# Two of four heads' softmax sums taken four slots at a time from SBUF, with a third buffer of logits and an earlier start of the statistics

## The chip, the cores and the metric

The kernel runs on one core of one Trainium2 chip. The metric is the device time of one execution in microseconds, and a version is given by the median of its runs. A profiled execution lies beside the timed ones: its span is what the trace covers, and its own device time is that span and the little around it.

## What is computed

The input is two images of 256 channels and 64 x 64 = 4096 positions. Two residual layers follow one another, each behind a group normalisation: a Mamba block (layer 0) and an attention of 8 heads with 32 channels each (layer 1). Everything is in float32.

```
# layer 0: x = x + mamba(group_norm(x))
# layer 1: x = x + attention(group_norm(x))
qkv = einsum('bchw,oc->bohw', x, qkv_w) + qkv_b
q, k, v = ...                                  # [b, head, 32, 4096] each
attn_logits = einsum('bhci,bhcj->bhij', q, k) / sqrt(32)
attn_weights = softmax(attn_logits, axis=-1)
out = einsum('bhij,bhcj->bhci', attn_weights, v)
```

The kernel leaves the maximum of the softmax out. It takes the exponential of the scaled logits, multiplies it with the values, sums the exponentials over the 4096 keys, and divides at the end. A check at the end of the kernel (`out_of_range`) sends inputs for which this would overflow to another routine, which does not run here.

## The kernel before

**Layer 0** is one stage for both images (`mamba_stage`). Its work is written as tasks with an engine, a due time and a cost, and a planner (`Plan`) orders them before anything is issued. What is written outside the planner is issued first, in the order of the text: on the queue of SP all weights and vectors (`load_rows`, `load_vec`, lines 327 to 354), about 3.7 MB. Then come the planner's tasks. `first` (line 313) loads one tile of 512 positions of an image into the ring `r_h` (five buffers) and takes `bn_stats` of it on VectorE; it is called for the 8 tiles of image 0 and of image 1. `group_norm` (line 405) makes the scales of the normalisation from an image's statistics, and `front(0)` starts the first tile of the Mamba block with a second load of the same input (`yn`, line 459).

**Layer 1** is done image by image (`attention_block`). `prepare` projects queries, keys and values and stores queries and keys in DRAM. Then comes the main loop, whose order is written out by hand. The heads go in two groups of four; a tile is one group and 512 queries; a slot is 128 keys of one tile. So a tile has 32 slots, an image has 2 x 8 x 32 = 512, and both have 1024. In a slot:

- TensorE makes logits for four heads as two halves of two heads (`logits`, line 964). A half fills a PSUM tile `s` of 128 x 1024[...]. The pool `ps_s` has two such buffers.
- ScalarE takes the exponential of a half in one instruction (`exponentials`, line 972) and writes it to SBUF (`e`, a ring of seven buffers).
- TensorE multiplies the four heads' exponentials with the values and accumulates over the tile in PSUM (`values`, line 981, tile `po`[...]).
- The exponentials are summed over the slots (`add_up`, line 990). The first half is added by VectorE to `acc`[...] (line 1002). The second half is added by GpSimd to `acc_p` in SBUF (line 1013); in the slots named by `SHARED` (every second one from slot 6, 13 in a tile) VectorE takes one head of it into `acc_2`[...] (lines 1008 and 1010), and GpSimd the other (line 1011).

At the end of a tile `finish` (line 1015) runs as a generator, one piece per slot beside the next tile's slots: copies of `acc` and `po` to SBUF, the sum over the 128 keys of a slot by a matmul with ones (line 1031), reciprocals, the product, and the residual.

With two logit buffers the loop is skewed by half a slot. In slot s ScalarE takes the second half of slot s and the first half of slot s + 1, and TensorE does the values of slot s - 1, then the second half of logits of slot s + 1 and the first half of slot s + 2:

```
                exponentials(s, 1)
                exponentials(s + 1, 0)
...
                values(s - 1)
...
            logits(s + 1, 1)
            logits(s + 2, 0)
            if s < S:
                add_up(s)
```

Of the kernel before, what the change touches and what calls it, by code (L numbers as in the profile page):

```python
# [11 lines left out]
F32 = mybir.dt.float32  # L12
F32R = mybir.dt.float32r
AF = mybir.ActivationFunctionType
ALU = mybir.AluOpType
# [4 lines left out]
P = 128  # L20
# [226 lines left out]
def mamba_stage(ctx, tc, xs, stats_out, consts, w, outs):  # L247
# [65 lines left out]
    def first(b, t, due):  # L313
        xt = Buf(r_h)
        add("SP", due, 0.8, lambda: nc.sync.dma_start(xt.tile, image_tile(xs[b], t)), [], [xt], lands=3.0)
        for k in range(KC):
            add(
                "DVE",
                due,
                0.7,  # L320
                lambda k=k: nc.vector.bn_stats(stats_in[b][:, k, t, :], xt.tile[:, k, :]),
                [xt],
                [stats_bufs[b][k * NT + t]],
            )

# [13 lines left out]
    w_in = load_rows("w_in", w["W_inT"], KC)  # L339
    conv_w = wp.tile([P, KD, TAPS], F32, name="conv_w")  # L340
    nc.sync.dma_start(conv_w, w["conv_w"].rearrange("(k p) o t -> p k (o t)", p=P))
    conv_b = load_vec("conv_b", w["conv_b"], KD)
    w_xp = load_rows("w_xp", w["W_xpT"], KD)
    b_dt = load_vec("b_dt", w["b_dt"], KD)
    d_vec = load_vec("d_vec", w["D"], KD)
    neg_a = wp.tile([P, KD, QUAD, NQ], F32, name="neg_a")
    nc.sync.dma_start(neg_a, w["A_log"].rearrange("p (k j q) -> p k j q", k=KD, j=QUAD))
    sum4 = wp.tile([P, PQ], F32, name="sum4")
    nc.sync.dma_start(sum4, w["sum4"])
    w_out = load_rows("w_out", w["W_outT"], KD)  # L350
    w_1 = load_rows("w_1", w["W1T"], KC)
    b_1 = load_vec("b_1", w["b1"], KH)
    w_2 = load_rows("w_2", w["W2T"], KH)
    b_2 = load_vec("b_2", w["b2"], KC)
# [5 lines left out]
    diag_d = wp.tile([P, KD, P], F32, name="diag_d")  # L360
    perm = r_yn.make()[:, 0, 0:P]
    nc.sync.dma_start(perm, w["perm"])
    for k in range(KD):
# [10 lines left out]
    pick = wp.tile([NS, NQ, P], F32R, name="pick")  # L374
    w_dt32 = r_yn.make()[:R, 0, :]
    nc.sync.dma_start(w_dt32, w["W_dtT"])
# [4 lines left out]
    pick32 = r_yn.make()[:NS, 0, :]  # L381
    nc.sync.dma_start(pick32, w["pick"])
# [5 lines left out]
    r_proj.make = itertools.cycle(projs).__next__  # L388


# [374 lines left out]
    for b in range(IMAGES):  # L765
        for t in range(NT):
            first(b, t, -60 + 10 * b)
    for b in range(IMAGES):
        for k in range(KC):
            group_norm(b, k, -48 + 10 * b)  # L770
    front(0)
# [42 lines left out]
def attention_block(ctx, tc, b, stats, consts, w, out, scratch, range_t):  # L814
# [14 lines left out]
    wp = ctx.enter_context(tc.tile_pool(name=f"l1w{b}", bufs=1))  # L829
    ps_s = ctx.enter_context(tc.tile_pool(name=f"l1pss{b}", bufs=2, space=PSUM))  # L830
    ps_a = ctx.enter_context(tc.tile_pool(name=f"l1psa{b}", bufs=1, space=PSUM))
    ps_2 = ctx.enter_context(tc.tile_pool(name=f"l1ps2{b}", bufs=1, space=PSUM))
# [109 lines left out]


    class Slot:
        pass

    S = KG * NT * NC
    SHARED = range(6, NC, 2)
    todo = {}
# [19 lines left out]
    def exponentials(s, half):  # L969
        if s < S:  # L970
            e = ep.tile([P, 2, T], F32, name="e")
            nc.scalar.activation(e, todo[s].s[half], AF.Exp, scale=SCALE)  # L972
            todo[s].e.append(e)

    def values(s):
        i, c = divmod(s, NC)
        g = i // NT
        if c == 0:
            tiles[i].po = ps_o.tile([P, T], F32, name="po")
        for h in range(4):  # L980
            nc.tensor.matmul(  # L981
                tiles[i].po[h * D : (h + 1) * D, :],
                lhsT=v[:, c, g * P + h * D : g * P + (h + 1) * D],
                rhs=todo[s].e[h // 2][:, h % 2, :],
                start=(c == 0),
                stop=(c == NC - 1),
            )
        del todo[s]

    def add_up(s):  # L990

        i, c = divmod(s, NC)
        tile_ = tiles[i]
        ea, eb = todo[s].e
# [7 lines left out]
        nc.vector.tensor_add(acc, acc, ea)  # L1002
        if c == 1:
            nc.gpsimd.tensor_add(acc_p, tile_.eb0, eb)  # L1004
        elif c in SHARED:
            if c == SHARED[0]:
                tile_.acc_2 = ps_2.tile([P, T], F32, name="acc_2", tag="a2")
                nc.vector.tensor_copy(tile_.acc_2, eb[:, 0, :])
            else:
                nc.vector.tensor_add(tile_.acc_2, tile_.acc_2, eb[:, 0, :])  # L1010
            nc.gpsimd.tensor_add(acc_p[:, 1, :], acc_p[:, 1, :], eb[:, 1, :])  # L1011
        else:
            nc.gpsimd.tensor_add(acc_p, acc_p, eb)  # L1013

    def finish(i):
# [34 lines left out]
    with tc.manual_schedule():  # L1050
        logits(0, 0)
        logits(0, 1)
        exponentials(0, 0)
        logits(1, 0)
# [201 lines left out]
```

## Time and profile before

| what | us |
|---|---|
| median of 3 runs (4609.26 to 4615.61) | 4610.98 |
| the profiled execution's own time | 4614.82 |
| its span | 4613.0 |

The stages, read from the busy time of the engines by stretch (us busy in each):

| stretch of the span, us | what runs | PE | VectorE | ScalarE | GpSimd |
|---|---|---|---|---|---|
| 0 to 45 | loads, statistics of both images | 0.0 | 27.2 | 1.5 | 2.7 |
| 45 to 112 | group norm, front of the first tiles | 56.0 | 12.1 | 35.9 | 10.2 |
| 112 to 2090 | Mamba block, both images | 1779.9 | 1804.7 | 1585.1 | 1906.8 |
| 2090 to 2194 | prepare, image 0 | 92.1 | 43.5 | 28.2 | 0.0 |
| 2194 to 3336 | attention, image 0 | 1142.0 | 889.2 | 989.9 | 978.8 |
| 3336 to 3452 | prepare, image 1 | 97.2 | 52.0 | 29.2 | 3.2 |
| 3452 to 4594 | attention, image 1 | 1142.0 | 887.2 | 989.4 | 977.8 |
| 4594 to 4613 | last tile's end, check | 2.4 | 9.4 | 0.0 | 3.6 |

A matmul's end is modelled in the trace and includes time in which it stands behind others, so TensorE's 1142.0 us in the attention stretches do not say that it always had work; the distance between the starts of matmuls does. GpSimd is the busiest engine of the Mamba block (1906.8 of 1978 us).

### The profile page before, as it was taken

Reading aid. Unit: us, or ns where it says so; the run is one execution under the profiler, and the core shown is the slowest. Engines: PE = TensorE matmul, PEld = TensorE weight load, DVE = VectorE, ACT = ScalarE, POOL = GpSimd, SP = SyncE. Lnnn points to the kernel's source line nnn. Section 1 sums busy time; section 2 is a strip of 40 time slices with the busy share of each in tenths; the row PEclk is TensorE's granted clock in tenths of the full one; section 3 lists DMA queues with packets and bytes.
Section 4 is the critical chain, followed back from the end, with each engine's and each line's share of the span. In section 5 each row is a group of like instructions: output and inputs, shape, how many; then the busy total and the mean of one; then the engine's idle time right before and its main releaser. Section 6 shows DMA issues by size and latency. Waiting matters only on the chain.

```text
span 4613.0 us, 55891 instructions
## 1 busy us (share of the span) xinstructions
PE 4311.6 (93%) x18530; PEld 1571.9 (34%) x18530; DVE 3725.3 (81%) x3980; ACT 3659.2 (79%) x4796; POOL 3883.1 (84%) x2251
## 2 busy tenths in 40 slices
PE   4799899999999999888999999999989999999998
PEld 2233333333333333324333333333343333333332
DVE  3999999999999999963777777777747777777777
ACT  3778888888888888752888888888828888888887
POOL 1999999999999999960888888888808888888887
PEclk9899999999999999989999999999999999999999
DMA  5333333333333333318210140101081101401000
GB/s 172 105 107 111 108 122 119 123 124 124 124 124 111 119 124 122 108 41 256 77 44 17 26 101 17 26 17 29 7 262 37 44 17 28 99 17 26 24 23 8
DMA packets 162329, 379.66 MB, mean 82 GB/s; under 512 B 23408, under 2 KB 41584, under 8 KB 153840
## 3 DMA queue, kind: packets, MB, share of 16 engines
q1 hardware_dynamic: 162032, 376.03, 26.6%
q8 instruction: 147, 2.41, 0.2%
q14 instruction: 150, 1.23, 0.1%
HBM read 282.64 MB, written 93.32 MB: 81 GB/s over the span
## 4 chain that ended last, share of the span: by engine, by line
PE 65%; POOL 11%; DVE 10%; issue 6%; ACT 3%; DMA 3%; SPq 0%; POOLq 0%; DVEq 0%; ACTq 0%
PE s L964 27%; PE po L981 22%; DVE h L721 6%; POOL h L727 6%; PE mm L403 6%; POOL dbu L716 3%; PE y L753 2%; PE mm L599 2%; PE mm L635 2%; PE s L887 1%; DVE bn L716 1%; DMA xn<-x_dram 1%; PE bn L403 1%; ACT da L710 1%; DMA dtu_rep<-dtu_dram 1%
## 5 line engine op out<-in xcount | busy, mean ns | idle before, releaser
L972 ACT ACTIVATE e<-s 128x1024 f32<-128x1024 f32 x2048 | 1987.1, 1022 | 305.2 <-PE s L964 305.0
L1002 DVE TENSOR_TENSOR acc<-acc,e 128x1024 f32<-128x1024 f32 x992 | 1219.4, 1229 | 407.5 <-ACT e L972 404.4
L1013 POOL TENSOR_TENSOR acc_p<-acc_p,e 128x1024 f32<-128x1024 f32 x544 | 1300.4, 2390 | 235.0 <-ACT e L972 222.5
L964 PE MATMUL s<-q,k 128*128 128x512 f32 x4096 | 1317.4, 435 | 3.8 <-ACT e L972 2.1
L727 POOL TENSOR_TENSOR h<-h,c 128x1024 f32<-128x1024 f32 x512 | 1206.5, 2370 | 15.4 <-ACT state L724 10.0
L981 PE MATMUL po<-e,v 128*32 128x512 f32 x8192 | 1092.0, 605 | 0.0
L964 PEld LDWEIGHTS s<-q,k 128*128 128x128 f32 x4096 | 614.0, 188 | 1120.2 <-ACT e L972 1114.5
L710 ACT ACTIVATE da<-dt_rep,neg_a 128x512 f32<-128x512 f32 x1024 | 691.3, 701 | 119.8 <-DVE h L721 98.0
L721 DVE TENSOR_TENSOR_SCAN h<-da,state,dbu 128x512 f32<-128x512 f32 x512 | 649.9, 1274 | 81.3 <-POOL dbu L716 72.1
L721 DVE TENSOR_TENSOR_SCAN h<-da,state,bn 128x512 f32<-128x512 f32 x512 | 647.6, 1265 | 13.7
L1011 POOL TENSOR_TENSOR acc_p<-acc_p,e 128x512 f32<-128x512 f32 x416 | 548.0, 1317 | 33.0 <-POOL acc_p L1013 0.6
L716 POOL TENSOR_TENSOR dbu<-dtu_rep,b 128x512 f32<-128x512 f32 x384 | 488.1, 1282 | 10.0 <-DMA dtu_rep<-dtu_dram 8.4
L234 ACT ACT_TABLE_LOAD x331 | 424.7, 1283 | 6.7 <-PEq L1246 0.7
L403 PE MATMUL bn<-proj,pick 112*128 112x512 f32 x512 | 307.6, 616 | 118.3 <-DVE h L721 117.9
L753 PE MATMUL y<-h,sum 128*32 128x512 f32 x2048 | 379.9, 638 | 40.2 <-POOL h L727 40.1
L716 DVE TENSOR_TENSOR bn<-dtu_rep,bn 128x512 f32<-128x512 f32 x512 | 348.9, 681 | 34.8 <-DMA dtu_rep<-dtu_dram 19.1
L1010 DVE TENSOR_TENSOR acc<-acc,e 128x512 f32<-128x512 f32 x384 | 268.7, 700 | 58.5 <-ACT e L972 37.8
L1004 POOL TENSOR_TENSOR acc_p<-e 128x1024 f32<-128x1024 f32 x32 | 76.4, 2387 | 273.5 <-ACT e L972 273.5
L981 PEld LDWEIGHTS po<-e,v 128*32 128x32 f32 x8192 | 161.6, 108 | 373.2 <-issue 361.9
L403 PE MATMUL mm<-yn,w_in 128*128 128x512 f32 x512 | 264.5, 642 | 10.0 <-ACT yn L492 4.5
L403 PE MATMUL mm<-xm,taps 128*128 128x512 f32 x512 | 235.5, 603 | 16.4 <-POOL xm L539 14.2
L403 PE MATMUL mm<-yn,w 128*128 128x512 f32 x512 | 239.1, 596 | 11.5 <-ACT z L587 10.2
(125 smaller groups left out, 3444.6 us busy)
## 6 DMA issues: line engine op xcount, KB each, us to landing
dt_rep<-dt_dram SPq DMA_DIRECT2D x128, 512.0 KB, 5.0
dtu_rep<-dtu_dram SPq DMA_DIRECT2D x128, 512.0 KB, 5.7
qk_dram<-halves SPq DMA_DIRECT2D x64, 512.0 KB, 5.9
q<-qk_dram SPq DMA_DIRECT2D x128, 256.0 KB, 4.8
k<-qk_dram SPq DMA_DIRECT2D x64, 512.0 KB, 7.6
b<-bc_dram SPq DMA_DIRECT2D x64, 256.0 KB, 3.0
c<-bc_dram SPq DMA_DIRECT2D x64, 256.0 KB, 4.1
dt_dram<-dt SPq DMA_DIRECT2D x64, 256.0 KB, 2.0
```

Source lines behind the costliest of these rows:

```text
L403: nc.tensor.matmul(out, lhsT=lhsT, rhs=rhs, start=(i == 0), stop=(i == len(pairs) - 1))
L710: nc.scalar.activation(da[j].tile, dt.tile[:, j, :], AF.Exp, scale=scale)
L716: engine.tensor_mul(out.tile, dtu.tile[:, j, :], rows.tile)
L721: nc.vector.tensor_tensor_scan(h.tile[:, j, :], da[j].tile, dbu.tile, initial, ALU.mult, ALU.add)
L727: nc.gpsimd.tensor_tensor(h.tile, h.tile, rows_c.tile.unsqueeze(1).to_broadcast([P, 2, T]), ALU.mult)
L753: nc.tensor.matmul(y.tile[j * PQ : (j + 1) * PQ, :], lhsT=sum4, rhs=pair[j // 2].h.tile[:, j % 2, :], start=False, stop=(qd == NQ - 1),)
L964: nc.tensor.matmul(ps[:, j, :], lhsT=keys[i // NT, kt][:, h, kj : kj + P], rhs=queries[i][:, h, :], start=True, stop=True)
L972: nc.scalar.activation(e, todo[s].s[half], AF.Exp, scale=SCALE)
L981: nc.tensor.matmul(tiles[i].po[h * D : (h + 1) * D, :], lhsT=v[:, c, g * P + h * D : g * P + (h + 1) * D], rhs=todo[s].e[h // 2][:, h % 2, :],
L1002: nc.vector.tensor_add(acc, acc, ea)
L1011: nc.gpsimd.tensor_add(acc_p[:, 1, :], acc_p[:, 1, :], eb[:, 1, :])
L1013: nc.gpsimd.tensor_add(acc_p, acc_p, eb)
```

## The change

In the attention:

- `acc` in PSUM is gone, and `ps_s` has three buffers of logits instead of two. The skew of half a slot goes with it: slot s takes both halves of its own exponentials, and TensorE makes both halves of slot s + 1.
- The first half's exponentials are no longer added slot by slot. Four slots' exponentials are written into one SBUF tile `chunk` of five parts of 128 x 1024 (two such tiles). After the fourth slot one `tensor_reduce` on VectorE adds the parts: the four new ones and part 0, the running sum of the chunks before. It writes its result into part 0 of the next chunk. The first reduction of a tile has four terms, the next six have five, and the last one, in `finish`, has five and writes to `acc_sb` directly. The read is made by `rearrange("p k h t -> p (h t) k")`: the innermost step goes from part to part, that is 1024 elements or 4096 bytes at a time.
- The ring `e` serves the second half alone and has five buffers instead of seven.
- `SHARED` has 15 slots of a tile instead of 13 (from slot 8 those whose number has the remainder 0, 2, 4, 5 or 6 by 8).
- `finish` copies `po` first, then reduces, and waits five slots instead of one before the matmul with ones.

At the start of the kernel:

- The loads and statistics of image 0 are issued before all weights, outside the planner. Image 1's stay tasks, with a later due time.
- `w_out`, `w_1` and `w_2` are loaded by one late task of the planner; some small loads change their places.

```diff
+    with tc.manual_schedule():
+        for t in range(NT):
+            first(0, t, 0)
...
+    def load_late():
+        for tile_, name in ((w_out, "W_outT"), (w_1, "W1T"), (w_2, "W2T")):
+            nc.sync.dma_start(tile_, w[name].rearrange("(k p) f -> p k f", p=P))
...
-        for t in range(NT):
-            first(b, t, -60 + 10 * b)
+        for t in range(NT if b else 0):
+            first(b, t, -30)
...
-            group_norm(b, k, -48 + 10 * b)
+            group_norm(b, k, -48 + 24 * b)
+    add("SP", -20, 2.4, load_late, [], [late_buf], lands=12.0)
...
-    ps_s = ctx.enter_context(tc.tile_pool(name=f"l1pss{b}", bufs=2, space=PSUM))
-    ps_a = ctx.enter_context(tc.tile_pool(name=f"l1psa{b}", bufs=1, space=PSUM))
+    ps_s = ctx.enter_context(tc.tile_pool(name=f"l1pss{b}", bufs=3, space=PSUM))
...
-    ep = ctx.enter_context(tc.tile_pool(name=f"l1e{b}", bufs=7))
+    CHUNK = 4
+    ep = ctx.enter_context(tc.tile_pool(name=f"l1e{b}", bufs=5))
+    ec = ctx.enter_context(tc.tile_pool(name=f"l1c{b}", bufs=2))
...
-    SHARED = range(6, NC, 2)
+    SHARED = [c for c in range(8, NC) if c % 8 in (0, 2, 4, 5, 6)]
...
     def exponentials(s, half):
-        if s < S:
+        c = s % NC
+        if half == 0:
+            if c % CHUNK == 0:
+                todo[s].chunk = todo.pop("chunk", None) or chunk()
+            else:
+                todo[s].chunk = todo[s - 1].chunk
+            e = todo[s].chunk[:, 1 + c % CHUNK]
+        else:
             e = ep.tile([P, 2, T], F32, name="e")
-            nc.scalar.activation(e, todo[s].s[half], AF.Exp, scale=SCALE)
-            todo[s].e.append(e)
+        nc.scalar.activation(e, todo[s].s[half], AF.Exp, scale=SCALE)
+        todo[s].e.append(e)
+
+    def chunk():
+        return ec.tile([P, 1 + CHUNK, 2, T], F32, name="chunk")
+
+    def sum_chunk(s, out):
+        first = 1 if s % NC < CHUNK else 0
+        terms = todo[s].chunk.rearrange("p k h t -> p (h t) k")[:, :, first:]
+        nc.vector.tensor_reduce(out.rearrange("p h t -> p (h t)"), terms, AX.X, ALU.add)
...
     def add_up(s):
...
+        if c % CHUNK == CHUNK - 1 and c < NC - 1:
+            todo["chunk"] = chunk()
+            sum_chunk(s, todo["chunk"][:, 0])
         if c == 0:
-            tile_.acc = ps_a.tile([P, 2, T], F32, name="acc")
             tile_.acc_p = p2.tile([P, 2, T], F32, name="acc_p")
-            nc.vector.tensor_copy(tile_.acc, ea)
             tile_.eb0 = eb
             return
-        acc, acc_p = tile_.acc, tile_.acc_p
-        nc.vector.tensor_add(acc, acc, ea)
+        acc_p = tile_.acc_p
...
-        acc = p1.tile([P, 3, T], F32, name="acc_sb")
-        nc.vector.tensor_copy(acc[:, 0:2, :], d.acc)
-        nc.vector.tensor_add(acc[:, 2, :], d.acc_2, d.acc_p[:, 0, :])
         po = p1.tile([P, T], F32, name="po_sb")
         nc.vector.tensor_copy(po, d.po)
+        acc = p1.tile([P, 3, T], F32, name="acc_sb")
+        sum_chunk(i * NC + NC - 1, acc[:, 0:2])
+        nc.vector.tensor_add(acc[:, 2, :], d.acc_2, d.acc_p[:, 0, :])
...
-        yield
+        yield 5
...
-                exponentials(s + 1, 0)
+                exponentials(s, 0)
...
+            logits(s + 1, 0)
             logits(s + 1, 1)
-            logits(s + 2, 0)
```

More of the change, by code (lines that the diff above doesn't have):

```diff
@@ L314, in first @@
         xt = Buf(r_h)
-        add("SP", due, 0.8, lambda: nc.sync.dma_start(xt.tile, image_tile(xs[b], t)), [], [xt], lands=3.0)
-        for k in range(KC):
[L317 to L324, printed above, removed]
+        load = lambda: nc.sync.dma_start(xt.tile, image_tile(xs[b], t))
+        stats = lambda k: nc.vector.bn_stats(stats_in[b][:, k, t, :], xt.tile[:, k, :])
+        if b == 0:
+            xt.tile = r_h.make()
+            load()
+            for k in range(KC):
+                stats(k)
+            return
+        add("SP", due, 0.8, load, [], [xt], lands=3.0)
+        for k in range(KC):
+            add("DVE", due, 0.7, lambda k=k: stats(k), [xt], [stats_bufs[b][k * NT + t]])
+    with tc.manual_schedule():
+        for t in range(NT):
+            first(0, t, 0)
     def load_rows(name, src, k):
@@ L338, in mamba_stage @@
     beta = load_vec("beta", w["beta"], KC)
-    w_in = load_rows("w_in", w["W_inT"], KC)
     conv_w = wp.tile([P, KD, TAPS], F32, name="conv_w")
@@ L342, in mamba_stage @@
     conv_b = load_vec("conv_b", w["conv_b"], KD)
+    w_in = load_rows("w_in", w["W_inT"], KC)
     w_xp = load_rows("w_xp", w["W_xpT"], KD)
     b_dt = load_vec("b_dt", w["b_dt"], KD)
-    d_vec = load_vec("d_vec", w["D"], KD)
     neg_a = wp.tile([P, KD, QUAD, NQ], F32, name="neg_a")
     nc.sync.dma_start(neg_a, w["A_log"].rearrange("p (k j q) -> p k j q", k=KD, j=QUAD))
+    w_dt32 = r_yn.make()[:R, 0, :]
+    nc.sync.dma_start(w_dt32, w["W_dtT"])
+    pick32 = r_yn.make()[:NS, 0, :]
+    nc.sync.dma_start(pick32, w["pick"])
+    d_vec = load_vec("d_vec", w["D"], KD)
+    perm = r_yn.make()[:, 0, 0:P]
+    nc.sync.dma_start(perm, w["perm"])
     sum4 = wp.tile([P, PQ], F32, name="sum4")
     nc.sync.dma_start(sum4, w["sum4"])
-    w_out = load_rows("w_out", w["W_outT"], KD)
-    w_1 = load_rows("w_1", w["W1T"], KC)
     b_1 = load_vec("b_1", w["b1"], KH)
-    w_2 = load_rows("w_2", w["W2T"], KH)
     b_2 = load_vec("b_2", w["b2"], KC)
@@ L360, in mamba_stage @@
     diag_d = wp.tile([P, KD, P], F32, name="diag_d")
-    perm = r_yn.make()[:, 0, 0:P]
-    nc.sync.dma_start(perm, w["perm"])
     for k in range(KD):
@@ L374, in mamba_stage @@
     pick = wp.tile([NS, NQ, P], F32R, name="pick")
-    w_dt32 = r_yn.make()[:R, 0, :]
-    nc.sync.dma_start(w_dt32, w["W_dtT"])
     for row in (0, LOW):
@@ L380, in mamba_stage @@
         nc.vector.tensor_sub(w_dt[rows, 1, :], w_dt32, w_dt[rows, 0, :].bitcast(F32))
-    pick32 = r_yn.make()[:NS, 0, :]
-    nc.sync.dma_start(pick32, w["pick"])
     nc.vector.tensor_copy(pick.rearrange("r q p -> r (q p)"), pick32)
@@ L388, in mamba_stage @@
     r_proj.make = itertools.cycle(projs).__next__
+    w_out, w_1, w_2 = (
+        wp.tile([P, k, C if name != "w_1" else HID], F32, name=name)
+        for name, k in (("w_out", KD), ("w_1", KC), ("w_2", KH))
+    )
+    late_buf = Buf()
+    def load_late():
+        for tile_, name in ((w_out, "W_outT"), (w_1, "W1T"), (w_2, "W2T")):
+            nc.sync.dma_start(tile_, w[name].rearrange("(k p) f -> p k f", p=P))
     state = wp.tile([P, IMAGES, KD, QUAD, NQ], F32, name="state")
@@ L987, in values @@
             )
-        del todo[s]
     def add_up(s):
@@ L993, in add_up @@
         tile_ = tiles[i]
-        ea, eb = todo[s].e
+        eb = todo[s].e[1]
+        if c % CHUNK == CHUNK - 1 and c < NC - 1:
+            todo["chunk"] = chunk()
+            sum_chunk(s, todo["chunk"][:, 0])
         if c == 0:
-            tile_.acc = ps_a.tile([P, 2, T], F32, name="acc")
             tile_.acc_p = p2.tile([P, 2, T], F32, name="acc_p")
-            nc.vector.tensor_copy(tile_.acc, ea)
             tile_.eb0 = eb
             return
-        acc, acc_p = tile_.acc, tile_.acc_p
-        nc.vector.tensor_add(acc, acc, ea)
+        acc_p = tile_.acc_p
         if c == 1:
@@ L1052, in attention_block @@
         logits(0, 1)
-        exponentials(0, 0)
-        logits(1, 0)
         s = 0
```

## Prediction

> **What bounds the kernel now.** I read the stages first, then the costliest groups, then the waits and TensorE's timeline in the attention, which takes half the span, and the timeline of the start.
>
> ```profile
> L972 ACT ACTIVATE e<-s 128x1024 f32<-128x1024 f32 x2048 | 1987.1, 1022 | 305.2 <-PE s L964 305.0
> L1002 DVE TENSOR_TENSOR acc<-acc,e 128x1024 f32<-128x1024 f32 x992 | 1219.4, 1229 | 407.5 <-ACT e L972 404.4
> L1013 POOL TENSOR_TENSOR acc_p<-acc_p,e 128x1024 f32<-128x1024 f32 x544 | 1300.4, 2390 | 235.0 <-ACT e L972 222.5
> ...
> L1011 POOL TENSOR_TENSOR acc_p<-acc_p,e 128x512 f32<-128x512 f32 x416 | 548.0, 1317 | 33.0 <-POOL acc_p L1013 0.6
> ...
> L1010 DVE TENSOR_TENSOR acc<-acc,e 128x512 f32<-128x512 f32 x384 | 268.7, 700 | 58.5 <-ACT e L972 37.8
> ```
>
> No engine but TensorE is full: ScalarE waits for logits (305 us), the adders wait for exponentials. The waits from 3560 to 4500 us name the partner:
>
> ```profile
> PEld s L964 <- ACT e L972: 457.2, 827, 0.8
> ...
> ACT e L972 <- PE s L964: 125.0, 421, 1.2
> ```
>
> Logits wait for the exponentials that free their buffer, and exponentials for logits: a loop through two buffers. TensorE's timeline shows its price:
>
> ```profile
> 4002.82 1.07 PE L981 MATMUL po<-e,v 128*32 128x512 f32 x8
> 4003.82 1.19 PE L964 MATMUL s<-q,k 128*128 128x512 f32 x4
> 4004.94 1.07 PE L981 MATMUL po<-e,v 128*32 128x512 f32 x8
> 4005.93 1.38 PE L964 MATMUL s<-q,k 128*128 128x512 f32 x4
> 4007.24 0.64 PE L981 MATMUL po<-e,v 128*32 128x512 f32 x4
> ```
>
> Slots last 2.12 us (4002.82 to 4004.94) and 2.30 us in turn. In the short one values (1.00) and four logits (1.12) follow each other closely; in the long one the second pair of logits came late. Value matmuls start at 3451.57 in the first tile of image 1 and at 4526.20 in the last: 71.64 us a tile of 32 slots, of which the sums of a finished tile make one slot 2.9 to 3.0 us. At the start:
>
> ```profile
> 22.83 6.03 DVE L321 BATCH_NORM_STATS2 stats_in<-h 128x6 f32<-128x512 f32 x10
> ...
> 37.06 8.05 DVE L321 BATCH_NORM_STATS2 stats_in<-h 128x6 f32<-128x512 f32 x12 [0.74 <-DMA h<-in_x]
> ...
> 45.02 0.59 DVE L412 BATCH_NORM_AGGREGATE gn<-stats_in 128x2 f32<-128x48 f32 x2
> ...
> 48.26 1.50 ACT L457 ACTIVATE yn<-yn,scales 128x512 f32<-128x512 f32 x2
> ```
>
> Image 0's scales wait until VectorE has taken image 1's statistics too, behind 3.7 MB of weights.
>
> [...] 512 elements take 676 ns, close to the 700 of an add:
>
> ```profile
> L1043 DVE TENSOR_REDUCE range_t<-r 128x1 f32<-128x512 f32 x32 | 21.6, 676 | 0.0
> ```
>
> [...] No strided read of such length is in the trace.
>
> **The change part by part.**
>
> *TensorE.* The instructions stay. With three buffers the first half of slot s+1's logits goes to the buffer of the exponential before the last slot's end, the second to that of this slot's first exponential, which ends long before. The values need the last slot's exponentials. ScalarE needs 1.94 us for its two (timeline), less than 2.12. So every slot can be a short one: 32 x 2.12 = 67.8, and the sums matmul adds 2.96 - 2.12 = 0.84: 68.7 us a tile. The gain is 71.6 - 68.7 = 2.9 a tile, 32 tiles: 93 us; I take 88, for the shorter first tiles. This is the floor; what follows says if it is reached.
>
> *VectorE, the reductions.* By the rows above an element costs (1229 - 700)/512 = 1.033 ns, so five terms (5120 elements) take 676 + 4608 x 1.033 = 5.44 us and four 4.38, if a strided element costs what a contiguous one does. That is a factor f = 1. Per tile: one of 4096 and seven of 5120 elements, 39,936 x 1.033 = 41.3 us x f, and 8 x 0.15 fixed = 1.2. It replaces 31 x 1.23 and two copies of 1.22: 40.5 us. So at f = 1 the reductions are no cheaper than the adds; they free PSUM. The 15 shared adds take 15 x 0.70 = 10.5 (before 9.1). `finish` keeps 7.9: copies and add 3 x 0.68, two maxima 1.36, reciprocals 4 x 0.94, residual 0.74. Sum 19.6 + 41.3 f. At f = 1 60.9 of 68.7 us, 89%: it hides behind TensorE. The queue is in order, so shared adds wait up to 5.4 us (2.6 slots) behind a reduction; `e` has five buffers, so ScalarE is not held. The next chunk's buffer was reduced four slots (8.5 us) earlier: no wait at f = 1, a wait of some 2 us per chunk at f = 2. Ends: `po` is copied first, so the next tile's values wait for nothing new; the matmul with ones, five slots (10.6 us) on, finds the sum made (1.0 + 0.7 + 5.4 + 0.7 = 7.8).
>
> [...] TensorE's floor holds to f = 1.19 (19.6 + 41.3 f = 68.7); the old tile time is reached at f = 1.26. I take f = 1[...]. This is the choice that the sign hangs on.
>
> *GpSimd.* 16 x 2.39 + 15 x 1.32 + 1.28 = 59.3 us a tile (before 61.4). Seven full adds run at the head of a tile against slots of 2.12: it falls 7 x 2.39 - 6 x 2.12 = 4.0 us behind and catches up; five buffers cover that.
>
> *Ends of the images.* Nothing hides the last tile's `finish`. Before, `acc` was copied at once and the matmul began 3.2 us after the last values' start (4593.93 to 4597.15). Now: values 1.0, copy 0.68, reduction 5.44, add 0.69: 7.8. Twice +4.6: +9.
>
> *Start.* SP issues eight loads of 0.5 MB first. At about 385 GB/s (DMA view, 0 to 125 us) 4.2 MB take 11 us, the first lands at some 5, the last statistics end near 17 us. Then SP goes through 15 vectors, `w_in` and small matrices at 0.5 us each, before the load of the first `yn`, which lands at about 25. So the normalisation that began at 48.3 begins at about 26. Behind it the chain is the old one, but on VectorE the scaling of `yn` stands behind statistics of image 1 whose loads follow the 2.5 MB of late weights, landing near 41 us, some 4 later than wanted. Gain 20 us, between 12 and 23. The Mamba stage runs at 98.5% of GpSimd, so its end moves with its start:
>
> ```profile
> 200.00:1000.00 800.00, 730.65 (x2185) 270.04 (x2182) 742.52 (x806) 658.84 (x1085) 788.23 (x498) 0.96 0.36 120
> ```
>
> The planner's order differs after that in detail; I cost it at 0, +-5. `prepare` has a third PSUM buffer too, but its slots stand at TensorE (10.3 us a period) or at stores: 0 to -5, taken 0.
>
> Sum: -88 - 20 + 9 = -99. On the profiled 4614.8 that is 4516; the median is 3.8 lower, so 4512.
>
> **Rivals.**
>
> *Rival 1, slower: the strided read.* Place: the reduction in SBUF; it decides from f = 1.26. VectorE becomes the bound, with tile time 19.6 + 41.3 f. At f = 1.5 this is 81.5 (+9.9 x 32 = 317 us), less 20, ends +18: about 4925. At f = 2 it is 102.2 (+30.6 x 32 = 979), start -20, ends +26: about 5596. [...] Against: no strided row in the trace[...].
>
> *Rival 2, little moves.* At 89% with instructions of 5.4 us VectorE may hold `e` or the chunk now and then, or f lies at 1.1 to 1.25, so that slots stay near 2.2 us; then the start and part of the attention remain: 4540 to 4625.
>
> *Rival 3, the loop stays.* If the alternation 2.12/2.30 came from a fixed cost of TensorE's switch between 128-row and 32-column work, the third buffer would give nothing in the long slots. Against: the late pair waits for ScalarE by name (457 us). Then only the start is gained: 4600.
>
> **How the numbers follow.** Forecast (f near 1, all slots short): 0.50, 4512, own range 4485 to 4550. Rivals 2 and 3 together: 0.10, of which 0.05 faster, 0.03 the same, 0.02 slower. Rival 1: 0.40. With 0.2% (9 us) as what a measurement can tell from no change: faster 0.55, same 0.03, slower 0.42. Half the chance lies on either side, so the range reaches from 4485 to the far end of rival 1, 5620.
>
> **What would show it.** Right: TENSOR_REDUCE of 128x1024 at about 5.4 us; every slot near 2.12; hardly a wait of logits for exponentials; group norm's aggregate near 17 us; VectorE near 89% in the attention. Wrong: reductions of 7 us and over, VectorE at 99%, exponentials and sums waiting for it, TensorE idle.

## The result, and the profile after

The changed kernel takes 5214.33 us (median of 4 runs, 5212.17 to 5214.41), the kernel before in the same session 4613.3 us: a ratio of 1.130, 95% interval 1.128 to 1.132. The profiled execution took 5214.3 us, its span is 5212.6.

The trace, cut at the first and the last value matmul of each image (us), says where the 600 us lie; e3 and e12 are experiments told of below (e3 adds neighbours in place of the terms of one sum; it is a measure, not a version to use):

| stretch | before | after | e3, contiguous read | e12, fastest usable version |
|---|---|---|---|---|
| start to first value matmul | 2194.08 | 2195.42 | 2193.93 | 2175.16 |
| image 0, first to last value matmul | 1141.44 | 1427.69 | 1098.22 | 1120.07 |
| to the first value matmul of image 1 | 116.05 | 130.39 | 124.32 | 117.19 |
| image 1, first to last value matmul | 1142.82 | 1428.11 | 1097.98 | 1121.33 |
| to the end | 18.65 | 30.94 | 24.11 | 24.15 |
| span | 4613.04 | 5212.55 | 4538.56 | 4557.90 |

The two attention stretches cost 571.5 us more, the ends of the images 26.6, and of the earlier start nothing is left at the first value matmul of this execution (+1.3). A tile takes 90.0 us instead of 71.6 (mean distance of the copies of `po` within an image). The costliest groups of the changed kernel, with different shapes kept apart (after the count: us busy, mean ns of one, then idle time before them and what ended it):

```profile
L1008 DVE TENSOR_REDUCE chunk<-chunk 128x1024 f32<-128x5120 f32 x192 | 1801.0, 9380 | 2.5 <-ACT chunk L998 2.5
...
L998 ACT ACTIVATE chunk<-s 128x1024 f32<-128x1024 f32 x1024 | 1051.2, 1027 | 896.5 <-DVE chunk L1008 543.3 <-PE s L983 267.6 <-DVE acc_sb L1008 85.1
...
L1008 DVE TENSOR_REDUCE chunk<-chunk 128x1024 f32<-128x4096 f32 x32 | 243.3, 7604 | 30.3 <-ACT chunk L998 30.3
```

A reduction of five terms takes 9.38 us, one of four 7.60. The difference is 1024 elements: (9380 - 7604) / 1024 = 1.734 ns an element, with some 0.5 us fixed. So it is in the main a price for each element read, not for each output, and it is 1.68 times the 1.033 ns that the kernel before pays for a contiguous element. The exponentials into a chunk wait for these reductions. The busy time in 800 us of attention (the columns are PE, PEld, VectorE, ScalarE, GpSimd, each with the number of its instructions, then the granted clock, and the share and GB/s of the DMA engines):

```profile
2400.00:3200.00 800.00, 679.71 (x3479) 253.77 (x3478) 793.70 (x293) 543.77 (x569) 522.37 (x284) 0.94 0.13 30
```

VectorE is at 99% (793.70 of 800), TensorE at 85%. The waits from 3560 to 4500 us, where logits and exponentials waited for each other before:

```profile
ACT chunk L998 <- DVE chunk L1008: 155.0, 53, 4.5
PEld s L983 <- ACT chunk L998: 138.4, 59, 7.2
```

A chunk's buffer that VectorE has not summed yet now holds ScalarE, and ScalarE holds the logits. In the timeline one sees both halves of the change at work:

```profile
4510.53 9.25 DVE L1008 TENSOR_REDUCE chunk<-chunk 128x1024 f32<-128x5120 f32 x1
...
4512.69 0.62 PE L1016 MATMUL po<-chunk,v 128*32 128x512 f32 x2
...
4514.82 0.62 PE L1016 MATMUL po<-chunk,v 128*32 128x512 f32 x2
...
4516.94 0.62 PE L1016 MATMUL po<-chunk,v 128*32 128x512 f32 x2
...
4519.87 1.02 ACT L998 ACTIVATE chunk<-s 128x1024 f32<-128x1024 f32 x1 [3.47 <-DVE chunk L1008]
```

From 4512.69 to 4516.94 slots follow one another every 2.13 and 2.12 us: the alternation of 2.12 and 2.30 is gone. Then the exponential of the next chunk's first slot stands for 3.47 us, until VectorE, which began its sum at 4510.53, is done.

At the start (the timeline's columns: start, us, instruction, and in brackets what its engine waited for):

```profile
16.30 0.58 DVE L427 BATCH_NORM_AGGREGATE gn<-stats_in 128x2 f32<-128x48 f32 x2
...
28.75 0.81 ACT L472 ACTIVATE yn<-yn,scales 128x512 f32<-128x512 f32 x1 [6.44 <-issue]
...
44.16 2.05 DVE L316 BATCH_NORM_STATS2 stats_in<-h 128x6 f32<-128x512 f32 x3 [6.29 <-DMA h<-in_x]
46.13 1.39 DVE L503 SCALAR_TENSOR_TENSOR yn<-yn,gamma,mm 128x512 f32<-128x512 f32 x2
```

The aggregate comes 28.7 us earlier than before (45.02), the first normalisation 19.5 us earlier (48.26). But the scaling of `yn` stands on VectorE behind statistics of image 1 whose loads landed late (6.29 us).

### The profile page after: what moved, and what is told of

Its sections match the earlier page's. It is cut to its first block, busy times and chain, and to the rows that moved or that the text cites. A ratio compares the mean times of both kernels' runs of the same rounds, so it can differ in the third digit from the quotient of the medians.

```text
span 5212.6 us, 53763 instructions
## 1 busy us (share of the span) xinstructions
PE 4473.1 (86%) x18530; PEld 1703.5 (33%) x18530; DVE 4785.9 (92%) x3244; ACT 3636.5 (70%) x4797; POOL 3806.2 (73%) x2251
## 5 line engine op out<-in xcount | busy, mean ns | idle before, releaser
L1008 DVE TENSOR_REDUCE chunk<-chunk 128x1024 f32<-128x5120 f32 (+1 forms) x224 | 2044.3, 9126 | 32.8 <-ACT chunk L998 32.8
L998 ACT ACTIVATE chunk<-s 128x1024 f32<-128x1024 f32 x1024 | 1051.2, 1027 | 896.5 <-DVE chunk L1008 543.3
L1046 POOL TENSOR_TENSOR acc_p<-acc_p,e 128x1024 f32<-128x1024 f32 x480 | 1148.1, 2392 | 278.5 <-ACT e L998 265.2
L983 PEld LDWEIGHTS s<-q,k 128*128 128x128 f32 x4096 | 714.4, 199 | 1502.5 <-issue 930.0
L1016 PE MATMUL po<-chunk,v 128*32 128x512 f32 x4096 | 1148.3, 641 | 28.4 <-DVE po_sb L1054 28.4
L1016 PE MATMUL po<-e,v 128*32 128x512 f32 x4096 | 1155.7, 645 | 0.0
L998 ACT ACTIVATE e<-s 128x1024 f32<-128x1024 f32 x1024 | 1049.4, 1025 | 0.2 <-issue 0.2
L1044 POOL TENSOR_TENSOR acc_p<-acc_p,e 128x512 f32<-128x512 f32 x480 | 622.3, 1296 | 581.3 <-ACT e L998 570.8
L1008 DVE TENSOR_REDUCE acc_sb<-chunk 128x1024 f32<-128x5120 f32 x32 | 299.6, 9361 | 0.0
L1016 PEld LDWEIGHTS po<-chunk,v 128*32 128x32 f32 x4096 | 151.4, 110 | 427.6 <-issue 384.3
```

Source lines behind the costliest of these rows:

```text
L983: nc.tensor.matmul(ps[:, j, :], lhsT=keys[i // NT, kt][:, h, kj : kj + P], rhs=queries[i][:, h, :], start=True, stop=True)
L1008: nc.vector.tensor_reduce(out.rearrange("p h t -> p (h t)"), terms, AX.X, ALU.add)
L1016: nc.tensor.matmul(tiles[i].po[h * D : (h + 1) * D, :], lhsT=v[:, c, g * P + h * D : g * P + (h + 1) * D], rhs=todo[s].e[h // 2][:, h % 2, :],
```

## Experiments

### What makes the reduction slow: e1, e2, e3, e8

**e1: the distance between the terms, by tile.** The same count of elements, `n` elements apart, each `n` on its own line (1012, 1014, ... 1026 for 1, 2, ... 1024):

```diff
-        terms = todo[s].chunk.rearrange("p k h t -> p (h t) k")[:, :, first:]
...
+        flat = todo[s].chunk[:, first:].rearrange("p k h t -> p (k h t)")
+        n = (1, 2, 4, 8, 16, 64, 256, 1024)[(s // NC) % 8]
+        terms = flat.rearrange("p (a k n) -> p a n k", n=n, k=5 - first)
```

> The changed kernel, with the same number of elements read by each reduction, but the distance between two elements that are summed set by the tile: 1, 2, 4, 8, 16, 64, 256 and 1024 elements (4 to 4096 bytes) in tiles 0 to 7, each on a line of its own; every exponential is still added once, but at distances below 1024 into the sum of another query, so the outputs are not the reference's. Theory A (the distance of the read sets the price): about 5.4 us for 5 terms at distance 1 and about 9.4 us at 1024, with the step somewhere between[...]. Theory B (a reduction in runs of five costs 1.73 ns an element whatever it reads): 9.4 us at all eight. Theory C (GpSimd's adds beside it slow the reduction): also 9.4 us at all eight, and only the run without these adds tells C from B.

VectorE's groups of e1, costliest first (lines 1012 to 1020 are distances of 1, 2, 4, 8, 16 elements; 1022, 1024 and 1026 are 64, 256 and 1024):

```profile
L1016 DVE TENSOR_REDUCE chunk<-chunk 128x1024 f32<-128x5120 f32 x24 | 232.6, 9691 | 0.0
L1018 DVE TENSOR_REDUCE chunk<-chunk 128x1024 f32<-128x5120 f32 x24 | 232.5, 9686 | 0.0
L1024 DVE TENSOR_REDUCE chunk<-chunk 128x1024 f32<-128x5120 f32 x24 | 225.0, 9376 | 0.2 <-ACT chunk L998 0.2
L1026 DVE TENSOR_REDUCE chunk<-chunk 128x1024 f32<-128x5120 f32 x24 | 225.0, 9374 | 0.6 <-ACT chunk L998 0.6
L1022 DVE TENSOR_REDUCE chunk<-chunk 128x1024 f32<-128x5120 f32 x24 | 224.8, 9369 | 0.0
L1020 DVE TENSOR_REDUCE chunk<-chunk 128x1024 f32<-128x5120 f32 x24 | 221.2, 9218 | 0.0
L1012 DVE TENSOR_REDUCE chunk<-chunk 128x1024 f32<-128x5120 f32 x24 | 131.4, 5475 | 19.5 <-ACT chunk L998 19.5
L1014 DVE TENSOR_REDUCE chunk<-chunk 128x1024 f32<-128x5120 f32 x24 | 131.1, 5464 | 13.2 <-ACT chunk L998 13.2
```

At 4 and 8 bytes 5.48 and 5.46 us; from 16 bytes on 9.2 to 9.7, at every distance tried. There is one step, between 8 and 16 bytes, and at 8 nothing of it is paid; distances in between (3 elements, 12 bytes) were not tried. Theory A holds; B falls. (The one run took 5053.52 us, a mixture of tiles.) The runs show where the step lies, and not what makes it.

**e2: without GpSimd's adds.** The two adds in `add_up` after a tile's first are left out:

```diff
-            nc.gpsimd.tensor_add(acc_p[:, 1, :], acc_p[:, 1, :], eb[:, 1, :])
-        else:
-            nc.gpsimd.tensor_add(acc_p, acc_p, eb)
```

> The changed kernel without GpSimd's running adds of the second two heads (all but the first add of each tile are left out, so two of the four sums are incomplete). Theory C (VectorE's reduction is slowed by GpSimd reading and writing SBUF beside it): the reduction of 5 terms falls from 9.38 to about 5.4 us and the kernel to 4500 to 4560 us. Theories A and B: it stays at 9.2 to 9.4 us; VectorE loses nothing, so the kernel stays at 5130 to 5215 us.

The group of reductions, and the busy time in the attention (GpSimd is the last engine):

```profile
L1008 DVE TENSOR_REDUCE chunk<-chunk 128x1024 f32<-128x5120 f32 x192 | 1783.2, 9287 | 3.1 <-ACT chunk L998 3.1
```

```profile
2400.00:3200.00 800.00, 685.59 (x3511) 256.62 (x3508) 793.79 (x298) 548.29 (x573) 33.01 (x18) 0.94 0.12 30
```

GpSimd is busy 33 of 800 us instead of 522, and the reduction takes 9.29 us instead of 9.38; the kernel took 5190.95 us in its one run. Theory C falls: GpSimd's adds beside the reduction cost it 1%.

**e3: the whole kernel with a contiguous read.**

```diff
-        terms = todo[s].chunk.rearrange("p k h t -> p (h t) k")[:, :, first:]
+        flat = todo[s].chunk[:, first:].rearrange("p k h t -> p (k h t)")
+        terms = flat.rearrange("p (o k) -> p o k", o=2 * T)
```

> The changed kernel, with each reduction reading the same 5120 (or 4096) elements one after the other: five neighbours are summed into one output, so the sums are those of other queries and the outputs are not the reference's. Theory A: 5.3 to 5.5 us for each reduction of 5 terms instead of 9.38; VectorE then needs about 61 of the 68.7 us that TensorE needs for a tile and no longer bounds it, and the kernel comes to 4500 to 4570 us, a ratio of 0.976 to 0.990 to the kernel before. Theories B and C: 9.4 us and 5214 us, a ratio of 1.13.

4539.67 us, ratio 0.983 (0.9815 to 0.9848). The reductions, and the busy time in the attention:

```profile
L1009 DVE TENSOR_REDUCE chunk<-chunk 128x1024 f32<-128x5120 f32 x192 | 1049.4, 5466 | 111.9 <-ACT chunk L998 111.8
```

```profile
2400.00:3200.00 800.00, 800.00 (x4564) 312.11 (x4564) 695.57 (x386) 722.66 (x746) 690.93 (x373) 1.00 0.14 35
```

5.47 us a reduction, VectorE at 87%, TensorE without a gap by its modelled ends, 68.68 us a tile. The distance of the read alone is worth 675 us, and turns the sign.

**e8: is it the reduction alone?** On the basis of e7 (below) a `tensor_copy` of one exponential tile, 128x1024, every fourth slot, read at `n` elements and written contiguously, by tile:

```diff
+            src = ea.rearrange("p h t -> p (h t)").rearrange("p (a k n) -> p a n k", k=8, n=n)
+            dst = junk.rearrange("p (a n k) -> p a n k", k=8, n=n)
+            if n == 1:
+                nc.vector.tensor_copy(dst, src)
...
```

> The kernel of the additions in SBUF, with one more VectorE instruction every fourth slot whose output nobody reads: a tensor_copy of an exponential tile, 128x1024, read at distances of 1, 2, 4, 8, 16, 32, 64 and 128 elements in tiles 0 to 7 (a line each) and written contiguously. If the price belongs to any VectorE read at 16 bytes and more: about 1.2 us at distances 1 and 2, and 1.2 + 1024 x 0.7 ns = 1.9 to 2.0 us at 4 and above. If it belongs to the reduction alone: about 1.2 us at all eight.

The lines of distance 2 and of distance 4 (ns: min/median/max, then first and last start):

```profile
L1026 DVE COPY junk<-e x32: 680/1764/2882, 2300.2 to 4991.8; 128x1024 f32<-128x1024 f32 x32
```

```profile
L1028 DVE COPY junk<-e x32: 1051/2163/3364, 2401.8 to 5095.2; 128x1024 f32<-128x1024 f32 x32
```

The medians mix in waits for GpSimd, so I read the copies beside which no GpSimd instruction ran, four for each distance: 680 ns at distances 1 and 2, 1063 at 4 and 8, 1007 at 16, 1082 at 32, 1244 at 64 and 128. A copy slows at the same place as the reduction, so the step is not the reduction's own. Its size is not the expected one: the contiguous copy is faster than I wrote (0.68 instead of 1.2 us, where an add of as many elements takes 1.23), and the step is (1063 - 680) / 1024 = 0.37 ns an element against (9691 - 5464) / 5120 = 0.83 in the reduction at the same distance. Whether it is the same price is open: what the copy loses may be part of its higher rate, since at 64 and 128 elements it takes about what an add does.

### What sums could be made instead: e6, e7, e9

**e6: the terms of a sum as neighbours.** Contiguous for the reduction, 20 bytes apart for ScalarE's writes and TensorE's reads:

```diff
-            e = todo[s].chunk[:, 1 + c % CHUNK]
+            e = todo[s].chunk[:, :, :, 1 + c % CHUNK]
...
-        return ec.tile([P, 1 + CHUNK, 2, T], F32, name="chunk")
+        return ec.tile([P, 2, T, 1 + CHUNK], F32, name="chunk")
...
+        nc.vector.tensor_reduce(out, todo[s].chunk[:, :, :, first:], AX.X, ALU.add)
```

> The changed kernel with the chunk laid out the other way round: the five values that one sum needs are neighbours (4 bytes apart), so the reduction reads contiguously, while ScalarE writes its exponentials, VectorE the running sum and TensorE reads its moving rows at a distance of 20 bytes. All kernels agree that the reduction of 5 terms then reads in about 5.5 us (its writes at 20 bytes are the unknown there). Theory D (only reads of VectorE pay for distances of 16 bytes and more): exponentials stay at 1.02 us, tiles at 68.7 us, kernel 4535 to 4560 us, ratio 0.983 to 0.989. Theory E (every engine pays about 0.7 ns for each element at such a distance): the exponential into the chunk takes 1.7 us, ScalarE needs 2.7 us a slot instead of 2.12 and bounds the tile at 86 us or more, kernel 5080 us or more, ratio 1.10 or more; TensorE's two value matmuls on the chunk may slow too.

5508.77 us, ratio 1.194 (1.192 to 1.196), slower than the change. The exponentials and value matmuls, those on the chunk beside those on `e`, which stays contiguous:

```profile
L998 ACT ACTIVATE chunk<-s 128x1024 f32<-128x1024 f32 x1024 | 2128.0, 2078 | 166.7 <-PE s L983 87.9
L1015 PE MATMUL po<-chunk,v 128*32 128x512 f32 x4096 | 2059.6, 1091 | 0.0
...
L998 ACT ACTIVATE e<-s 128x1024 f32<-128x1024 f32 x1024 | 1099.2, 1073 | 0.0
L1015 PE MATMUL po<-e,v 128*32 128x512 f32 x4096 | 1079.3, 605 | 0.0
```

ScalarE's write at 20 bytes takes 2.08 us instead of 1.07, TensorE's read 1.09 us instead of 0.605. Theory E had the direction, and its price was too small (1.0 ns an element instead of 0.7 for ScalarE). A tile takes 99.0 us. The trace speaks for TensorE as what sets it, not ScalarE as the theory had it: in the slot at 2603.99 us the logits start 1.93 us after the values (1.00 in e3) and the next values 1.13 us later, 3.06 in all, and from 2400 to 3200 us no wait of TensorE for ScalarE is listed, while ScalarE is busy for 757 of 800 us. No run separates the two.

**e7: one addition a slot, in SBUF.** Three buffers of logits, no chunk:

```diff
+            tile_.acc = p2.tile([P, 3, T], F32, name="acc_sb")
+            tile_.ea0 = ea
...
+        both = tile_.acc[:, 0:2, :]
+        nc.vector.tensor_add(both, tile_.ea0 if c == 1 else both, ea)
```

> The changed kernel without chunks: three buffers of logits and the start stay, and the sum of the first two heads is again one addition a slot, now into a tile in SBUF instead of PSUM (with ten buffers of exponentials). Theory F (an addition of two SBUF inputs costs VectorE what the one with a PSUM input did, 1.23 us, and GpSimd keeps its 2.39): VectorE needs 31 x 1.23 + 10.5 + 7.2, about 56 of 68.7 us a tile; TensorE bounds; nothing waits for the last stores before the first exponential: 4515 to 4545 us, ratio 0.978 to 0.986. Theory G (with two SBUF inputs it contends with GpSimd): if the additions take turns with GpSimd's 59 us a tile, both are late, GpSimd's adds rise well above 2.39 us or VectorE's above 1.6 us, and the tile takes over 72 us: above 4620 us.

5285.76 us, ratio 1.146 (1.144 to 1.147). The additions of both engines:

```profile
L1017 DVE TENSOR_TENSOR acc_sb<-acc_sb,e 128x1024 f32<-128x1024 f32 x960 | 2230.3, 2323 | 174.7 <-ACT e L988 138.1 <-DVE acc_sb L1017 1.9
...
L1028 POOL TENSOR_TENSOR acc_p<-acc_p,e 128x1024 f32<-128x1024 f32 x480 | 1500.5, 3126 | 244.2 <-ACT e L988 212.9
...
L1026 POOL TENSOR_TENSOR acc_p<-acc_p,e 128x512 f32<-128x512 f32 x480 | 986.7, 2056 | 37.6
```

VectorE's addition takes 2.32 us instead of the 1.23 it took with a PSUM input, GpSimd's 3.13 and 2.06 instead of 2.39 and 1.32. The 30 additions of this size into `acc_sb` beside which no GpSimd instruction runs (28 of them the first of a tile) take 1.21 us. Theory G is right: beside each other, VectorE's addition with two SBUF inputs and GpSimd's addition both take longer. So the change's `tensor_reduce` had a ground, since it avoids this price (9.38 us beside GpSimd's adds, 9.29 without them in e2; the change made the two attention stretches 571.5 us longer, e7 651.9); it paid another. One thing was not as expected: the first exponential of each image waits for stores here too, 13.9 us for both.

**e9: pairs.** In e1 terms 8 bytes apart cost the reduction no more than neighbours (5.46 and 5.48 us). Theory H is that in such pairs each engine takes what it takes on contiguous data. The terms of a sum lie 8 bytes apart here, and the streams of ScalarE and TensorE come in runs of 8 bytes, 40 bytes from run to run:

```diff
-            e = todo[s].chunk[:, 1 + c % CHUNK]
+            e = todo[s].chunk[:, :, :, 1 + c % CHUNK, :]
...
+        nc.scalar.activation(e, pairs(ps) if half == 0 else ps, AF.Exp, scale=SCALE)
...
-        return ec.tile([P, 1 + CHUNK, 2, T], F32, name="chunk")
+        return ec.tile([P, 2, T // 2, 1 + CHUNK, 2], F32, name="chunk")
...
+        terms = todo[s].chunk.rearrange("p h u k n -> p (h u) n k")[:, :, :, first:]
+        nc.vector.tensor_reduce(out.rearrange("p h u n -> p (h u) n"), terms, AX.X, ALU.add)
```

> The changed kernel with the five terms of a sum 8 bytes apart instead of 4096: a chunk holds pairs of neighbouring queries, the five pairs of one place one after the other[...]. ScalarE writes and TensorE reads pairs at a distance of 40 bytes, the reduction reads at 8. Theory H[...]: reduction 5.47 us as at distance 2 in the first run, exponential into the chunk 1.03 us and its value matmuls 0.605 us as with contiguous data; tiles of 68.7 us; as the contiguous run, 4530 to 4548 us, ratio 0.982 to 0.986. Theory J (any break in a contiguous stream costs ScalarE or TensorE, say half of what 20 bytes did): exponential 1.55 us, ScalarE 2.6 us a slot, tiles of 82 us or more, 4960 us or more, ratio above 1.07.

4584.02 us, ratio 0.993 (0.9917 to 0.9944): 0.7% faster than the kernel before. The groups on the chunk:

```profile
L999 ACT ACTIVATE chunk<-s 128x1024 f32<-128x1024 f32 x1024 | 1146.8, 1120 | 179.8 <-PE s L983 98.2
L1020 PE MATMUL po<-chunk,v 128*32 128x512 f32 x4096 | 1141.0, 634 | 0.0
...
L1012 DVE TENSOR_REDUCE chunk<-chunk 128x1024 f32<-128x5120 f32 x192 | 1049.4, 5466 | 122.7 <-ACT chunk L999 122.7
```

The reduction takes 5.47 us, as theory H has it. But the exponential takes 1.12 us instead of 1.02 and the value matmuls 634 ns instead of 605, and a tile 70.16 us instead of 68.68. So H is right for VectorE and nearly so for the two others; the time is 36 us above its range. The tile follows TensorE: from the start of the values at 2600.78 us to the next logits it takes 1.04 us instead of 1.00 in e3, and a slot 2.16 to 2.17 instead of 2.12. What the exponential's 0.1 us is was not tried; its read of PSUM is written in pairs here too.

### The start and the ends of the images: e4, e5, e10, e11, e12

**e4 and e5: the two parts apart.** The hunks of the change, all of those ahead of the attention in e4, all of the others in e5, each on the kernel before. Their first lines:

```diff
# e4
+    with tc.manual_schedule():
+        for t in range(NT):
+            first(0, t, 0)
...
# e5
+    ps_s = ctx.enter_context(tc.tile_pool(name=f"l1pss{b}", bufs=3, space=PSUM))
...
```

> The kernel before with the start of the change alone (image 0's statistics loaded first, the other loads reordered, three weights loaded late); attention as before. In the changed kernel the first scaling of yn was 13.8 us early, and yet the first value matmul of attention came at 2195.4 us against 2194.1. Theory S1 (the Mamba stage gives the gain back, by its own pace or by another order): first value matmul at 2193 to 2197 us and the kernel at 4605 to 4618 us, ratio 0.998 to 1.001. Theory S2 (the gain reaches the end of the Mamba stage and something at the switch to attention in the changed kernel took it): first value matmul at about 2180 us and the kernel at 4595 to 4602 us, ratio 0.996 to 0.998.

> The kernel before with the attention part of the change alone; the start as before. If the two parts add up and the start gains nothing: 5205 to 5222 us, ratio 1.127 to 1.133. If the start is worth its 14 us: 5222 to 5236 us.

e4: 4605.09 us against 4612.28, ratio 0.9986 (0.9978 to 0.9994), first value matmul at 2186.43, 7.7 us early. Neither S1 nor S2 is quite right: the start is worth some 7 us, not 14 and not 0 (the time still lies within S1's range, the first value matmul between the two). e5: 5218.88 us, ratio 1.131 (1.130 to 1.133), in the range for a start that gains nothing; but its interval overlaps that of the change (1.128 to 1.132), so the two cannot tell 7 us from 0. In the profiled execution of the changed kernel nothing is left of the gain at the first value matmul, and one wait from 2150 to 2200 us has a part in this (us in all, times, longest):

```profile
ACT L998 <- DMA qk_dram<-halves: 6.7, 1, 6.7
```

The first chunk lies in SBUF where `prepare` had its tile `halves`, and must wait until that is stored. Logits begin at 2184.33 and the first exponential at 2193.19. In the kernel before these two are 0.85 us apart. Image 1 has the same wait, 7.1 us. The wait belongs to the attention part and not to the start: e5 has it with the old start (14.2 us for both images), and its first value matmul comes at 2196.25, 2.2 us later than before.

**e10: the first chunk elsewhere.** As e9, with one of the two chunk buffers allocated ahead of `prepare`:

```diff
+    ec0 = ctx.enter_context(tc.tile_pool(name=f"l1c{b}", bufs=1))
...
-    ec = ctx.enter_context(tc.tile_pool(name=f"l1c{b}", bufs=2))
+    ec1 = ctx.enter_context(tc.tile_pool(name=f"l1d{b}", bufs=1))
+    ecs = itertools.cycle((ec0, ec1))
```

> As the run with pairs, and the first chunk's buffer is set aside ahead of the projections, so that it doesn't lie over the tile whose stores to DRAM end last. Theory K (the 6.7 and 7.1 us in which the changed kernel's first exponential of each image waited for these stores are on the path): 12 to 14 us less than the run with pairs, 4517 to 4536 us, ratio 0.979 to 0.983, and the wait is gone. Theory L (something else is as late, such as the queries and keys that are loaded just then): the wait goes to another releaser, and the time stays within 4 us of the run with pairs. If pairs cost (theory J), the difference is still told by the first exponential.

4580.28 us, ratio 0.992 (0.9905 to 0.9932), 3.7 us less than e9: theory L in time, though not with the releaser that it gives as an example. The wait went to the next in line: the second exponential, into the first buffer of `e`, now stands 4.4 and 5.1 us for the same stores. So the first value matmul comes 7.5 us earlier than in e9 (2184.66 against 2192.12), and the two attention stretches are 3.2 and 3.3 us longer.

**e11: the late weights behind image 1's loads**, on e4:

```diff
-    add("SP", -20, 2.4, load_late, [], [late_buf], lands=12.0)
+    add("SP", -12, 2.4, load_late, [], [late_buf], lands=12.0)
```

> The kernel before with the start of the change alone, and the three late weights due at -12 instead of -20, so that SP issues them after all of image 1's loads instead of ahead of the last three. Theory M (the loads behind late weights are what the start lost on its way to Mamba's end): the first scaling of yn by gamma comes at 39 to 42 us instead of 45.8, the first scan at 100 to 103 instead of 106.0, and the first value matmul about 5 us earlier than with the start alone (2186.4): 2179 to 2183; kernel 4596 to 4603 us, ratio 0.996 to 0.998. Theory N (the planner's other order and the pace of the Mamba stage decide): the scaling is earlier, but scan and value matmul stay within 2 us of the start alone, ratio 0.998 to 0.999.

4600.13 us against 4613.61, ratio 0.997 (0.9958 to 0.9982). The scaling of `yn`, which came at 45.78 in e4:

```profile
39.28 1.41 DVE L503 SCALAR_TENSOR_TENSOR yn<-yn,gamma,mm 128x512 f32<-128x512 f32 x2 [0.18 <-ACT mm L495]
```

It is 6.5 us earlier, the first scan 6.9 us (99.08 instead of 106.01), the last matmul into the Mamba block's `y` ends 4.0 earlier (2031.79 instead of 2035.78), and the first value matmul comes 3.8 earlier (2182.66, the late end of theory M's range). Theory M. These are single executions, and executions with the same start differ by up to 6.3 us at the end of `y` (below); but e12, with the same late weights, has 2029.68, and both lie ahead of all ten executions with the weights due at -20 (2034.64 to 2040.91).

**e12: all together.** e10, with two of the five buffers of `e` also ahead of `prepare`, and the weights due at -12:

```diff
+    ep0 = ctx.enter_context(tc.tile_pool(name=f"l1f{b}", bufs=2))
...
-    ep = ctx.enter_context(tc.tile_pool(name=f"l1e{b}", bufs=5))
...
+    ep1 = ctx.enter_context(tc.tile_pool(name=f"l1e{b}", bufs=3))
+    eps = itertools.cycle((ep0, ep0, ep1, ep1, ep1))
```

> The run with pairs and an early first chunk buffer, with two of the five buffers of the other heads' exponentials also set aside ahead of the projections, and the late weights due at -12. If the waits of 4.4 and 5.1 us of the second exponential of each image for stores are on the path: 9 us less than the 4580 us of that run, 4566 to 4575, and up to 5 less again if the start's loads matter to the end: 4560 to 4575 us, ratio 0.988 to 0.991. If not: 4576 to 4584 us.

4562.52 us, ratio 0.989 (0.9873 to 0.9903), within the range for both gains. No exponential waits for a store any more. The two edits are not separated by a run; in the traces the last matmul into `y` ends 8.0 us earlier than in e10 (2037.66 there), and the attention stretches are 4.5 and 3.6 us shorter (1124.60 and 1124.92 there), about what the second exponentials had waited. This version is 51 us faster than the kernel before and 652 us faster than the change. It stays behind e3 in its tiles (70.16 against 68.68 us) and ahead of it at the start.

## Why the prediction was wrong, by its steps

**The step that failed is "I take f = 1".** Measured, f is 1.68. The text had the right place and the right point from which it decides (1.26). But no row of the profile carried a price for a strided read: f = 1 was the author's estimate, and so were rival 1's 1.5 and 2. e1 shows that the price is there from 16 bytes on (9.22 to 9.69 us) and not at 8 (5.46); e3 shows that the distance of this read alone decides the sign (ratio 0.983 against 1.130). Rival 1 came true, between its two prices.

**VectorE's sum was right.** 19.6 + 41.3 f gives 89.0 us a tile at f = 1.68; measured 90.0. Two small errors about cancel in this: the eight reductions take 73.3 us where the sum has 70.6 at this f, and neighbouring instructions overlap by some 2.4 us a tile (the add at 3007.38 us starts 0.10 us before the reduction from 2998.05 on, of 9.43 us, is over). At f = 1 it gave 89% of VectorE; e3 has 87%.

**TensorE's floor was right.** 68.7 us a tile; e3 has 68.68. Its two attention stretches are 43.2 and 44.8 us shorter, 88.1 in all where the sum had 88. Every slot of e3 has the same switch between 128-row and 32-column work, so rival 3 falls. The change also took the skew of half a slot away; whether the two buffers alone, without the skew, made the long slots was not tried.

**The wait for the next chunk's buffer** was priced at some 2 us a chunk at f = 2. The text's own sum asks for more: once VectorE is the bound, what it needs beyond TensorE's 68.7 us must be waited out somewhere, (102.2 - 68.7) / 8 = 4.2 us a chunk at f = 2 and 2.5 at 1.68. The row of the exponentials has (543.3 + 85.1) / 256 = 2.45 us a chunk.

**The ends of the images** were +9. With the contiguous read (e3) they are 8.3 and 5.5, 13.7 in all. The reduction at the end of an image was well sized (4.6 predicted; the matmul with ones starts 8.6 us after the last slot's values instead of 3.5). Most of the rest lies between the images, in `prepare`, taken at 0: nothing in the sum asked over which old tile the new chunks would lie. e12, whose exponentials do not wait, has 117.19 there against 124.32.

**The start** was 20, between 12 and 23. Its first events came about as written (16.30 and 28.75 us; 17 and 26 foretold). Then the gain shrank: 19.5 us at the first normalisation, 13.8 at the scaling of `yn`, 8.3 at the projection `w_xp` (85.72 to 77.38), 5.6 at the first scan (111.77 to 106.14). The first loss is the late loads, which e11 shows: foretold as some 4 us, it was 6.3. The second lies in the planner's order, "at 0, +-5": between the first activation of `u` and `w_xp` TensorE now does 12 matmuls of `w_in` instead of 8, image 1's group norm and 4 more with `lnmat`; this was read from the trace and not tried alone. At the end of the last matmul into `y` the ten profiled executions with the start as changed lie between 2034.64 and 2040.91 and the two with the old one at 2045.05 and 2045.96: 7.1 us in the mean, with up to 6.3 us between executions with the same start. The changed kernel's own is the latest of the ten and gains 4.1 us. From there to its first value matmul, with the wait for the stores on the way, it takes 5.5 us longer than the kernel before (154.5 against 149.0); e5, with the same wait, takes 1.3 us longer. What makes that difference stays open.

So at f = 1 the sum would have come out 28 us low (4512 against 4539.67 in e3), most of it from the start (20) and the ends (5).

## What to carry to other kernels

Before a sum is moved into SBUF, ask of each engine that touches the tile how far apart the elements lie that it takes one after the other. Single fp32 elements 16 bytes or more apart cost 1.7 to 1.8 times the time in VectorE's reduction (9.22 to 9.69 us against 5.48, e1); 20 bytes apart they cost 1.8 to 1.9 times in ScalarE's writes (2078 ns against 1073) and TensorE's reads (1091 against 605, e6). Elements 8 bytes apart cost nothing in the reduction (5.46 us, e1), and pairs of neighbours 40 bytes apart cost 5 to 10% on the two others (1120 ns against 1019, 634 against 605, e9). A layout that suits one reader may charge the writer and the other readers more than it saves (e6). And a new tile inherits the last reader of the SBUF under it: a pool that opens behind a stage with late stores can put them ahead of its first instruction (6.7 and 7.1 us here).

## What the runs showed of the hardware

- The reduction's price is a step and not a slope: 5.46 us at 8 bytes, 9.69 at 16, 9.37 at 4096 (e1).
- It is not one price: 0.73 to 0.83 ns an element in e1's reductions, 0.32 to 0.39 in a copy up to 32 elements apart and 0.55 from 64 on (e8), 1.0 in ScalarE's writes at 20 bytes (e6: 2078 against 1073 ns for 1024).
- A `tensor_copy` of 128x1024 within SBUF takes 0.68 us alone, and up to 2.88 us beside GpSimd's adds in e8.
